# Five states of h·C on GpSimd in pairs, and the last stage in place

## The chip, the cores and the metric

The kernel runs on one core of one Trainium2 chip. The metric is the device time of one launch in microseconds (us), taken as the median of several runs. The engines are called as in the profile: PE (TensorE, the matrix engine; PEld is its weight load), ACT (ScalarE), DVE (VectorE), POOL (GpSimd) and SP (SyncE, which here issues all the DMAs).

## The reference

The input x is 8 images of 56x56 pixels with 192 channels, all in fp32. Two layers are applied, each as x + f(group_norm(x)).

Layer 0 is an attention with depthwise convolutions in front of its projections: 3 heads of 64, queries from all 3136 pixels, keys and values from a grid of 28x28.

Layer 1 is a two-dimensional selective scan. A projection gives 384 inner channels and a gate z. The inner channels go through a depthwise 3x3 convolution and a SiLU. Then four directions k (by rows, by columns, and both reversed) each run a recurrence with 16 states n for each channel d along the 3136 pixels l:

```python
def step(h, inp):
    u_l, d_l, B_l, C_l = inp
    dA = jnp.exp(d_l[..., None] * A)
    dBu = d_l[..., None] * B_l[:, :, None, :] * u_l[..., None]
    h = dA * h + dBu
    y = jnp.sum(h * C_l[:, :, None, :], axis=-1)
    return (h, y)
```

delta, B and C are projections of the input itself. The four y are put back into image order and summed, together with a skip term, normed over the channels, multiplied by silu(z), and projected back to 192 channels.

## The kernel before, in words

**Tiles.** The 384 inner channels lie in NJ = 3 blocks of 128 partitions. The 3136 pixels of an image are cut into NCH = 7 chunks of T = 448. A "step" is one chunk in one direction of one image: 8 x 4 x 7 = 224 steps, 28 to an image ("batch"). In a step the 16 states follow each other; the list `todo` holds all pairs (step i, state n). Chunks of the two reversed directions run from the last to the first, and each image ends with direction 2.

**A state of a step.**

- `row_loads`: SP loads row B_n of the chunk into all partitions (tile bb, 3 buffers) and, for states that POOL finishes, row C_n (tile cb, 2 buffers).
- `inputs_made`: POOL multiplies delta·u (du_s) by B into a tile h of 128 x 1344 (L1123). There are HBUFS = 7 of these tiles.
- `decays`: ACT makes da = exp(delta·A) in PSUM, once for each channel block (L1137, 2 buffers).
- `scans`: DVE scans the three blocks in place in h (L1154). `carries` copies the last column to the next chunk (newc, L1176).
- For 13 states, y gets h·C by way of PE and ACT. `turned`: PE transposes h in four parts of 112 pixels, three transposes each (ht, L1200). `scaled`: ACT copies each part with C as the scale of its partition (g, L1216, four for a state). `back`: PE transposes them back, adding into y in PSUM (L1234).
- For the three states in BY_POOL = (2, 7, 12), `by_pool` lets POOL do it: h·C for the three channel blocks (L1252; the first goes into tile yp, the others stay in h), and the addition of the second and third to yp (L1256). `summed` then has PE add yp to y by a matmul with the identity for each block (L1271). yp has one buffer.
- y is a single PSUM buffer of three banks. `evicted`: DVE adds it to yacc, which holds all 3136 pixels (L1288; with the skip term for direction 0, L1286), and y is free for the next step.

**Around a step.** `prepared` makes the delta of the coming step (L1063 to L1082 on PE, ACT and DVE), and POOL multiplies it by u (L1086). `skips` loads the skip input of the next image into yacc as soon as a chunk of yacc has been read. `finish` is the last stage of an image, one `part` for each chunk, from the last chunk to the first: the mean over channels by PE (L949), its subtraction into a tile yc (L951), square, variance, norm, gate (the product with silu(z) on POOL, L986), the output projection on PE (L996) and the store. `read[c]`, set in it, is what `skips` waits for. `front` and `x_proj` are layer 0 and the projections of layer 1 of the next image; they run beside the scans of the present one.

**The order.** Each of these functions is a generator. A planner (`Sched`) runs them all while the program is built: with a fixed cost for each operation it keeps a clock for each engine and gives the next place to the operation that could start earliest, less a rank. The order on each engine is thus fixed; on the chip the engines wait for each other by semaphores. Two limits steer it. `pace` ties the PE time spent on front to the number of states scanned. `ending` makes the last stage urgent while the count of `read` lags behind the chunks that are ready:

```python
def ending():
    done = sum(len(r) for r in yread.values())
    b, c = divmod(at["chunk"], NDIR * NCH)
    come = b * NCH + max(c - (NDIR - 1) * NCH, 0)
    return 1e9, 1e9 if done < come - 1 or done < b * NCH else 0.0
```

Where PE would have nothing to do, a filler puts in small matmuls with zeros (L1367).

Of the kernel before, what the change touches and what calls it, by code (L numbers as in the profile page):

```python
# [36 lines left out]
R = 12  # L37
NR = R + 2 * NST
NDIR = 4
BY_POOL = (2, 7, 12)  # L40
EPS = 1e-5
CAP = 60.0
HBUFS = 7
LEAD = 3


# [224 lines left out]
def kernel(  # L271
# [661 lines left out]
    def finish(b, gate, read):  # L933

        m = made[b]
        wz = yield c1("wz2", [CP, NB, DIN])
        yield from scaled_weights(wz.ap, wz.c[0], 1, m["rstd"], m["k_gn"])

        def part(c):
            cols = slice(c * T, (c + 1) * T)  # L940
            yv = yacc[:, :, cols]
            yield gate(c)
            yc = yield c1("yc", [128, NJ, T], parts=4)
            xt = yield c1("xt3", [CP, NB, T])
            yield from dma([m["k_x1"][c]], xt.c, 5.0, xt.ap, m["x1d"][:, :, cols])
            pmn = yield bank()
            for j in range(NJ):
                yield PE, t_mm(T), [k_y[c]], pmn.c if j == NJ - 1 else []
                nc.tensor.matmul(pmn.ap[:, :T], lnones, yv[:, j], start=(j == 0), stop=(j == NJ - 1))  # L949
            yield DVE, t_dve(NJ * T), pmn.c + [k_y[c]], [yc.c[0]]  # L950
            nc.vector.tensor_tensor(yc.ap, yv, pmn.ap[:, :T].unsqueeze(1).to_broadcast([128, NJ, T]), ALU.subtract)  # L951
            pmn.free()
            read[c] = True
            sz = yield c1("sz", [128, NJ, T], parts=NJ + 2)
            yield ACT, t_act(NJ * T), [yc.c[0]], [sz.c[0]]
            nc.scalar.activation(sz.ap, yc.ap, AF.Square)
            pvr = yield bank()
            for j in range(NJ):
                yield PE, t_mm(T), [sz.c[0]], pvr.c if j == NJ - 1 else []
                nc.tensor.matmul(pvr.ap[:, :T], lnones, sz.ap[:, j], start=(j == 0), stop=(j == NJ - 1))  # L960
            k1, k2 = Cell(), Cell()
            yield ACT, t_act(T), pvr.c, [k1]
            nc.scalar.activation(pvr.ap[:, :T], pvr.ap[:, :T], AF.Ln, bias=eps)
            yield ACT, t_act(T), [k1] + pvr.c, [k2]
            nc.scalar.activation(pvr.ap[:, :T], pvr.ap[:, :T], AF.Exp, scale=-0.5)
            for j in range(NJ):
                yield DVE, t_dve(T), [k2, yc.c[0]] + pvr.c, [yc.c[2]] if j == NJ - 1 else []
                nc.vector.scalar_tensor_tensor(yc.ap[:, j], yc.ap[:, j], lnw[:, j], pvr.ap[:, :T], ALU.mult, ALU.mult)
            pvr.free()
            for j in range(NJ):  # L970
                yield ACT, t_act(T), [yc.c[2]], [yc.c[1]] if j == NJ - 1 else []
                nc.scalar.activation(yc.ap[:, j], yc.ap[:, j], AF.Identity, bias=lnb[:, j])
            for j in range(NJ):
                pz = yield bank()
                yield PE, 2 * t_mm(T), xt.c + wz.c, pz.c
                for bl in range(NB):
                    nc.tensor.matmul(pz.ap[:, :T], wz.ap[:, bl, j * 128:(j + 1) * 128], xt.ap[:, bl],
                                     start=(bl == 0), stop=(bl == NB - 1))
                yield DVE, t_dve(T), pz.c + [m["k_nb"], k2], [sz.c[1 + j]]
                nc.vector.tensor_scalar(sz.ap[:, j], pz.ap[:, :T], m["nbias"][:, NJ + j:NJ + j + 1], None, ALU.add)  # L980
                pz.free()
            yield ACT, t_act(NJ * T) + 2.6, sz.c[1:1 + NJ], [sz.c[1 + NJ]]
            nc.scalar.activation(sz.ap, sz.ap, AF.Silu)
            nc.scalar.preload_act_table_set(EXP_LN)
            yield POOL, t_pool(NJ * T), [yc.c[1], sz.c[1 + NJ]], [yc.c[3]]
            nc.gpsimd.tensor_tensor(yc.ap, yc.ap, sz.ap, ALU.mult)  # L986
            sz.free()
            ot = yield c1("ot", [TP, SUB, C], parts=2)
            for s2_ in range(SUB // 2):
                po = yield bank()  # L990
                for i in range(2):
                    s = 2 * s2_ + i
                    tok = slice(s * TP, (s + 1) * TP)
                    yield PE, 3 * t_mm(C) + 0.25, [yc.c[3]] + xt.c, po.c if i else []
                    for j in range(NJ):
                        nc.tensor.matmul(po.ap[:TP, i * C:(i + 1) * C], yc.ap[:, j, tok], outpw[:, j],  # L996
                                         start=(j == 0), stop=False)
                    for bl in range(NB):
                        nc.tensor.matmul(po.ap[:TP, i * C + bl * CP:i * C + (bl + 1) * CP], xt.ap[:, bl, tok],
                                         ident[:CP, :CP], is_transpose=True, start=False, stop=(bl == NB - 1))  # L1000
                yield ACT, t_act(2 * C), po.c, [ot.c[s2_]]
                nc.scalar.copy(ot.ap[:, 2 * s2_:2 * s2_ + 2].rearrange("p s c -> p (s c)"), po.ap[:TP, :2 * C])
                po.free()
            yc.free()
            xt.free()
            yield from dma(ot.c, [], 4.5, out[b, cols, :].rearrange("(s p) c -> p s c", p=TP), ot.ap, [ot])

        for c in reversed(range(NCH)):
            yield from part(c)
        wz.free()  # L1010
# [4 lines left out]
    for b in range(nb):  # L1015

        for k in (0, 1, 3, 2):
            order = range(NCH) if k < 2 else range(NCH - 1, -1, -1)
            steps += [(b, k, c, i) for i, c in enumerate(order)]
    todo = [(i, n) for i in range(len(steps)) for n in range(NST)]  # L1020

    def view(t, j, k, c):

# [78 lines left out]
    def row_loads():  # L1102
        for i, n in todo:
            b, k, c, _ = steps[i]
            yield lambda: i in chunks
            m = made[b]
            cols = slice(c * T, (c + 1) * T)
            bb = yield s3("bb", [128, T])
            yield from dma([m["k_rows"][k, c]], bb.c, 3.2, bb.ap, m["rows"][k][R + n, cols].partition_broadcast(128))
            brow[i, n] = bb  # L1110
            if n in BY_POOL:
                cbr = yield s2("cb", [128, T])
                yield from dma([m["k_rows"][k, c]], cbr.c, 3.2, cbr.ap,
                               m["rows"][k][R + NST + n, cols].partition_broadcast(128))
                crow[i, n] = cbr
# [63 lines left out]
    def y_of(i):  # L1179

        if i not in ys:
            t = yield ry
            free = Cell()
            free.w = t.c[0].r
            at["y"] = i
            ys[i] = dict(t=t, free=free, on=False, left=[(NST - len(BY_POOL)) * SUB + 1] * NJ)
        return ys[i]

    def turned():

        for i, n in todo:
            if n in BY_POOL:
                continue
            yield lambda: (i, n) in states
            h = states[i, n][0]
            for s in range(SUB):
                ht = yield rht
                yield PE, t_turn(128), h.c[1:1 + NJ], ht.c
                for j in range(NJ):
                    nc.tensor.transpose(ht.ap[:TP, j * 128:(j + 1) * 128], h.ap[:, j, s * TP:(s + 1) * TP], ident)  # L1200
                turns[i, n, s] = ht
            over(i, n)

    turns, gs, yps = {}, {}, {}

    def scaled():
        for i, n in todo:
            if n in BY_POOL:
                continue
            for s in range(SUB):  # L1210
                yield lambda: (i, n, s) in turns
# [9 lines left out]

    def back():
        for i, n in todo:
            if n in BY_POOL:
                continue
            for s in range(SUB):
                yield lambda: (i, n, s) in gs
# [12 lines left out]
    def by_pool():  # L1240

        for i, n in todo:
            if n not in BY_POOL:
                continue
            yield lambda: (i, n) in states and (i, n) in crow and i in news
            h, cbr = states[i, n][0], crow.pop((i, n))
            if n == BY_POOL[0]:
                yp = yield s1("yp", [128, NJ, T], parts=NJ)
            to = yp if n == BY_POOL[0] else h
            for j in range(NJ):  # L1250
                yield POOL, t_pool(T), [h.c[1 + j], news[i].c[n]] + cbr.c, [to.c[j]] if to is yp else [h.c[1 + NJ + j]]
                nc.gpsimd.tensor_tensor(to.ap[:, j], h.ap[:, j], cbr.ap, ALU.mult)  # L1252
# [2 lines left out]
                yield POOL, t_pool(NJ * T), h.c[1 + NJ:] + yp.c, yp.c  # L1255
                nc.gpsimd.tensor_tensor(yp.ap, yp.ap, h.ap, ALU.add)  # L1256
            over(i, n)
            if n == BY_POOL[-1]:
                yps[i] = yp

    def summed():

        for i in range(len(steps)):
            yield lambda: i in yps
            yp = yps.pop(i)
            y = yield from y_of(i)
            yield lambda: y["left"][0] < (NST - len(BY_POOL)) * SUB
            for j in range(NJ):
                yield PE, t_mm(T), [yp.c[j]], []
                y["left"][j] -= 1  # L1270
                nc.tensor.matmul(y["t"].ap[:, j, :T], ident, yp.ap[:, j], start=False, stop=(y["left"][j] == 0))  # L1271
            yp.free()
# [166 lines left out]
```

## Time and profile before

| | |
|---|---|
| time, median of 3 runs | 19163.19 us (19162.22 to 19167.43) |
| profiled execution, its own time | 19161.15 us |
| its span, first to last instruction | 19159.4 us |
| granted PE clock, mean | 0.98 |
| busy: PE / DVE / ACT / POOL | 17257.6 / 14540.1 / 15414.1 / 15248.7 us |
| bytes moved by DMA | 1662 MB, 87 GB/s |

A profile page shows one execution. A group of instructions is a line of the kernel, an engine, an operation and its tiles (out<-in), with its count, its busy time, the mean duration of one, and the time that the engine stood idle before it, with what ended that wait. "issue" means that the profile shows nothing that was waited for. Matmuls are pipelined and an fp32 matmul leaves two records, a transpose one, so counts of PE and its busy share say less than those of the other engines. Views by window give the busy time of each engine in a stretch of the span.

### The profile page before, as it was taken

What the parts mean: (1) busy time and instruction counts of PE and PEld (TensorE: products, weight loads), DVE (VectorE), ACT (ScalarE), POOL (GpSimd) and SP (SyncE); (2) the same over time, 40 slices, a digit from 0 to 9 for tenths busy, and PEclk for the clock granted to TensorE, in tenths of its full rate; (3) what the DMA queues carried; (4) which work ended last, traced back from release to release, by engine and by line L of the source; (5) the groups of instructions that cost most, each with busy time, mean ns of one, the idle gap of its engine ahead of it and who ended that gap; (6) DMA issues with size and microseconds to landing.
All of it is one profiled execution on the core that took longest, in us unless ns stands there. A gap on an engine that the chain in (4) does not pass through costs nothing. (4 is left out here: it accounts for less than half of the span.)

```text
span 19159.4 us, 294576 instructions
## 1 busy us (share of the span) xinstructions
PE 17257.6 (90%) x105374; PEld 12258.8 (64%) x105374; DVE 14540.1 (76%) x19156; ACT 15414.1 (80%) x28166; POOL 15248.7 (80%) x6380
## 2 busy tenths in 40 slices
PE   8799988999889998899999999999998999988888
PEld 4466666666666666666666666666666666667776
DVE  2377777777777777777877777777787777778887
ACT  2478888788877888788887888878888788888887
POOL 0388888788877888788887888878888788889997
PEclk9899999999999999999999999999999999999999
DMA  1322223222332233322333223332233222332222
GB/s 51 116 79 72 89 90 111 76 74 87 98 110 72 76 94 95 104 76 73 99 97 98 75 79 94 101 94 75 78 94 115 82 75 78 93 110 75 75 76 63
DMA packets 1071987, 1662.15 MB, mean 87 GB/s; under 512 B 162244, under 2 KB 1054392, under 8 KB 1067448
## 3 DMA queue, kind: packets, MB, share of 16 engines
q1 hardware_dynamic: 1070520, 1643.29, 28.3%
q8 instruction: 835, 13.68, 0.3%
q14 instruction: 632, 5.18, 0.1%
HBM read 1455.13 MB, written 187.74 MB: 86 GB/s over the span
## 5 line engine op out<-in xcount | busy, mean ns | idle before, releaser
L1154 DVE TENSOR_TENSOR_SCAN h<-da,newc,h 128x448 f32<-128x448 f32 x9216 | 10121.3, 1137 | 2016.7 <-ACT da L1137 1150.6
L1123 POOL TENSOR_TENSOR h<-du_s,bb 128x1344 f32<-128x1344 f32 x3584 | 10834.3, 3051 | 883.6 <-PE ht L1200 644.8
L1216 ACT ACTIVATE g<-ht,ct_s 112x384 f32<-112x384 f32 x11648 | 6534.5, 577 | 1522.9 <-PE ht L1200 1430.9
L1137 ACT ACTIVATE da<-dl_s,acoef 128x448 f32<-128x448 f32 x10752 | 6758.4, 637 | 869.0 <-DVE h L1154 689.5
L1234 PE MATMUL y<-ident,g 112*128 112x112 f32 x34944 | 5481.1, 271 | 888.7 <-ACT g L1216 722.1
L1234 PEld LDWEIGHTS y<-ident,g 112*128 112x128 f32 x34944 | 3799.5, 143 | 3596.0 <-ACT g L1216 2874.9
L1200 PE MATMUL ht<-ident,h 128*112 128x128 f32 x34944 | 5652.8, 277 | 244.8 <-DVE h L1154 77.1
L1200 PEld LDWEIGHTS ht<-ident,h 128*112 128x112 f32 x34944 | 4017.1, 135 | 924.7 <-issue 413.5
L1252 POOL TENSOR_TENSOR h<-h,cb 128x448 f32<-128x448 f32 x1344 | 1492.5, 1141 | 1204.8 <-issue 1076.4
L1086 POOL TENSOR_TENSOR du_s<-dl_s,du_s 128x1344 f32<-128x1344 f32 x224 | 681.5, 3043 | 1662.5 <-DVE dl_s L1082 1529.8
L1154 DVE TENSOR_TENSOR_SCAN h<-da,h 128x448 f32<-128x448 f32 x1536 | 1608.3, 1079 | 432.3 <-ACT da L1137 280.1
L1367 PE MATMUL y<-zeros 128*128 128x64 f32 x13790 | 1886.8, 270 | 0.0
L1367 PEld LDWEIGHTS y<-zeros 128*128 128x128 f32 x13790 | 1804.9, 197 | 14.2 <-issue 14.2
L1256 POOL TENSOR_TENSOR yp<-yp,h 128x1344 f32<-128x1344 f32 x448 | 1367.1, 3052 | 7.6
L451 PE MATMUL bank<-xa,dg 128*128 128x440 f32 (+2 forms) x3024 | 1303.5, 538 | 72.6 <-ACT g L1216 46.1
L755 PE MATMUL bank<-qT,kT 128*112 128x448 f32 x2352 | 1099.1, 558 | 91.9 <-ACT pT L705 49.4
L764 PE MATMUL bank<-pT,vt 112*128 112x448 f32 x2352 | 1004.1, 545 | 79.6 <-ACT pT L705 55.5
L451 PE MATMUL bank<-band,dgq 96*96 96x440 f32 (+3 forms) x2016 | 830.3, 534 | 47.9 <-ACT g L1216 27.2
L705 ACT ACTIVATE pT<-bank,nsh 112x448 f32<-112x448 f32 x1176 | 743.8, 635 | 115.8 <-PE bank L755 100.9
L1252 POOL TENSOR_TENSOR yp<-h,cb 128x448 f32<-128x448 f32 x672 | 747.7, 1146 | 1.8 <-DVE h L1154 1.8
L1070 DVE SCALAR_TENSOR_TENSOR dl_s<-prep,e 128x448 f32<-128x448 f32 x672 | 410.1, 610 | 444.3 <-ACT e L1068 443.9
L1063 PE MATMUL prep<-dts,dtw 128*128 128x448 f32 x1344 | 653.5, 568 | 99.0 <-DVE dl_s L1082 65.4
(152 smaller groups left out, 12559.5 us busy)
## 6 DMA issues: line engine op xcount, KB each, us to landing
bb<-rows SPq DMA_DIRECT2D x3584, 224.0 KB
cb<-rows SPq DMA_DIRECT2D x672, 224.0 KB
xt<-x1d SPq DMA_DIRECT2D x224, 336.0 KB
du_s<-xch SPq DMA_DIRECT2D x112, 672.0 KB
du_s<-xcw SPq DMA_DIRECT2D x112, 672.0 KB
xch<-xv SPq DMA_DIRECT2D x24, 1568.0 KB
xcw<-xw SPq DMA_DIRECT2D x168, 224.0 KB
xs<-xch SPq DMA_DIRECT2D x56, 672.0 KB
```

The source lines that it names most:

```text
L451: nc.tensor.matmul(out[:, o0:o1, a:b], lhs, img(lo, hi)[:, :, a + dx - 1:b + dx - 1], start=(t == TAPS[0]), stop=(t == TAPS[-1]))
L755: nc.tensor.matmul(ps.ap[:TP, :T], kts[h][:, kb * TP:(kb + 1) * TP], qh.ap, start=True, stop=True)
L764: nc.tensor.matmul(po.ap[:, :T], vt[:, kb, g:g + 2, :].rearrange("p g d -> p (g d)"), pts[kb].ap, start=(kb == 0), stop=(kb == NKB - 1))
L1123: nc.gpsimd.tensor_tensor(h.ap, du.ap, bb.ap.unsqueeze(1).to_broadcast([128, NJ, T]), ALU.mult)
L1137: nc.scalar.activation(da.ap[:, :T], dl.ap[:, j], AF.Exp, scale=acoef[:, k * NJ + j, n:n + 1])
L1154: nc.vector.tensor_tensor_scan(h.ap[:, j, rev], da.ap[:, 0:T][:, rev], h.ap[:, j, rev], news[i - 1].ap[:, j, n:n + 1] if ci else 0.0, ALU. ...
L1200: nc.tensor.transpose(ht.ap[:TP, j * 128:(j + 1) * 128], h.ap[:, j, s * TP:(s + 1) * TP], ident)
L1216: nc.scalar.activation(g.ap, ht.ap[:TP, :DIN], AF.Copy, scale=ct.ap[:, s, n:n + 1])
L1234: nc.tensor.matmul(y["t"].ap[:, j, s * TP:(s + 1) * TP], g.ap[:, j * 128:(j + 1) * 128], ident[:TP, :TP], is_transpose=True, start=(n == 0 ...
L1252: nc.gpsimd.tensor_tensor(to.ap[:, j], h.ap[:, j], cbr.ap, ALU.mult)
L1256: nc.gpsimd.tensor_tensor(yp.ap, yp.ap, h.ap, ALU.add)
L1367: nc.tensor.matmul(ybanks[:, 0, T:T + FILL], zeros, zeros[:, :FILL], start=False, stop=False)
```

## The change

BY_POOL becomes two sets of groups. Steps of every image but the last use ((2, 5), (8, 10), (13,)); steps of the last image use ((2, 7), (12,)). Within a group, the first h·C goes into yp, the second is added to it, and with the last of the group yp is handed to PE, which adds it to y; `summed` now runs once for each group. The states that POOL finishes are left out of `turned`, `scaled` and `back`.

The last stage no longer has the tile yc: it works in place in its chunk of yacc (yv), and `read[c]` is set after the last output matmul instead of after the subtraction. The tile h, which has the size of yc, gets an eighth buffer.

```diff
-BY_POOL = (2, 7, 12)
+BY_POOL = (((2, 7), (12,)), ((2, 5), (8, 10), (13,)))
-HBUFS = 7
+HBUFS = 8
...
             yield gate(c)
-            yc = yield c1("yc", [128, NJ, T], parts=4)
+            kc = [Cell() for _ in range(4)]
...
-            nc.vector.tensor_tensor(yc.ap, yv, pmn.ap[:, :T].unsqueeze(1).to_broadcast([128, NJ, T]), ALU.subtract)
+            nc.vector.tensor_tensor(yv, yv, pmn.ap[:, :T].unsqueeze(1).to_broadcast([128, NJ, T]), ALU.subtract)
             pmn.free()
-            read[c] = True
...
-            nc.gpsimd.tensor_tensor(yc.ap, yc.ap, sz.ap, ALU.mult)
+            nc.gpsimd.tensor_tensor(yv, yv, sz.ap, ALU.mult)
...
-                    yield PE, 3 * t_mm(C) + 0.25, [yc.c[3]] + xt.c, po.c if i else []
+                    yield PE, 3 * t_mm(C) + 0.25, [kc[3]] + xt.c, po.c + [k_y[c]] if i else []
...
-            yc.free()
+            read[c] = True
             xt.free()
...
+    by = [BY_POOL[b < nb - 1] for b, *_ in steps]
+    by = [{n: (n == g[0], n == g[-1]) for g in groups for n in g} for groups in by]
...
-            if n in BY_POOL:
+            if n in by[i]:
                 cbr = yield s2("cb", [128, T])
...
-            ys[i] = dict(t=t, free=free, on=False, left=[(NST - len(BY_POOL)) * SUB + 1] * NJ)
+            ys[i] = dict(t=t, free=free, on=False, left=[(NST - len(by[i])) * SUB + sum(z for _, z in by[i].values())] * NJ)
...
-            if n == BY_POOL[0]:
+            first, last = by[i][n]
+            if first:
                 yp = yield s1("yp", [128, NJ, T], parts=NJ)
-            to = yp if n == BY_POOL[0] else h
+            to = yp if first else h
...
-            if n == BY_POOL[-1]:
-                yps[i] = yp
+            if last:
+                yps.append((i, yp))
...
-        for i in range(len(steps)):
-            yield lambda: i in yps
-            yp = yps.pop(i)
+        for _ in range(sum(z for d in by for _, z in d.values())):
+            yield lambda: yps
+            i, yp = yps.pop(0)
             y = yield from y_of(i)
-            yield lambda: y["left"][0] < (NST - len(BY_POOL)) * SUB
+            yield lambda: y["on"]
```

More of the change, by code (lines that the diff above doesn't have):

```diff
@@ L949, in part @@
                 nc.tensor.matmul(pmn.ap[:, :T], lnones, yv[:, j], start=(j == 0), stop=(j == NJ - 1))
-            yield DVE, t_dve(NJ * T), pmn.c + [k_y[c]], [yc.c[0]]
-            nc.vector.tensor_tensor(yc.ap, yv, pmn.ap[:, :T].unsqueeze(1).to_broadcast([128, NJ, T]), ALU.subtract)
+            yield DVE, t_dve(NJ * T), pmn.c + [k_y[c]], [kc[0]]
+            nc.vector.tensor_tensor(yv, yv, pmn.ap[:, :T].unsqueeze(1).to_broadcast([128, NJ, T]), ALU.subtract)
             pmn.free()
-            read[c] = True
             sz = yield c1("sz", [128, NJ, T], parts=NJ + 2)
-            yield ACT, t_act(NJ * T), [yc.c[0]], [sz.c[0]]
-            nc.scalar.activation(sz.ap, yc.ap, AF.Square)
+            yield ACT, t_act(NJ * T), [kc[0]], [sz.c[0]]
+            nc.scalar.activation(sz.ap, yv, AF.Square)
             pvr = yield bank()
@@ L966, in part @@
             for j in range(NJ):
-                yield DVE, t_dve(T), [k2, yc.c[0]] + pvr.c, [yc.c[2]] if j == NJ - 1 else []
-                nc.vector.scalar_tensor_tensor(yc.ap[:, j], yc.ap[:, j], lnw[:, j], pvr.ap[:, :T], ALU.mult, ALU.mult)
+                yield DVE, t_dve(T), [k2, kc[0]] + pvr.c, [kc[2]] if j == NJ - 1 else []
+                nc.vector.scalar_tensor_tensor(yv[:, j], yv[:, j], lnw[:, j], pvr.ap[:, :T], ALU.mult, ALU.mult)
             pvr.free()
             for j in range(NJ):
-                yield ACT, t_act(T), [yc.c[2]], [yc.c[1]] if j == NJ - 1 else []
-                nc.scalar.activation(yc.ap[:, j], yc.ap[:, j], AF.Identity, bias=lnb[:, j])
+                yield ACT, t_act(T), [kc[2]], [kc[1]] if j == NJ - 1 else []
+                nc.scalar.activation(yv[:, j], yv[:, j], AF.Identity, bias=lnb[:, j])
             for j in range(NJ):
@@ L984, in part @@
             nc.scalar.preload_act_table_set(EXP_LN)
-            yield POOL, t_pool(NJ * T), [yc.c[1], sz.c[1 + NJ]], [yc.c[3]]
-            nc.gpsimd.tensor_tensor(yc.ap, yc.ap, sz.ap, ALU.mult)
+            yield POOL, t_pool(NJ * T), [kc[1], sz.c[1 + NJ]], [kc[3]]
+            nc.gpsimd.tensor_tensor(yv, yv, sz.ap, ALU.mult)
             sz.free()
@@ L993, in part @@
                     tok = slice(s * TP, (s + 1) * TP)
-                    yield PE, 3 * t_mm(C) + 0.25, [yc.c[3]] + xt.c, po.c if i else []
+                    yield PE, 3 * t_mm(C) + 0.25, [kc[3]] + xt.c, po.c + [k_y[c]] if i else []
                     for j in range(NJ):
-                        nc.tensor.matmul(po.ap[:TP, i * C:(i + 1) * C], yc.ap[:, j, tok], outpw[:, j],
+                        nc.tensor.matmul(po.ap[:TP, i * C:(i + 1) * C], yv[:, j, tok], outpw[:, j],
                                          start=(j == 0), stop=False)
@@ L1191, in turned @@
         for i, n in todo:
-            if n in BY_POOL:
+            if n in by[i]:
                 continue
@@ L1202, in turned @@
             over(i, n)
-    turns, gs, yps = {}, {}, {}
+    turns, gs, yps = {}, {}, []
     def scaled():
         for i, n in todo:
-            if n in BY_POOL:
+            if n in by[i]:
                 continue
@@ L1223, in back @@
         for i, n in todo:
-            if n in BY_POOL:
+            if n in by[i]:
                 continue
@@ L1242, in by_pool @@
         for i, n in todo:
-            if n not in BY_POOL:
+            if n not in by[i]:
                 continue
```

## The prediction

> **What bounds the kernel now.** I read the page's part 1 first. PE 90%, ACT 80%, POOL 80%, DVE 76%: no engine is full over the span, and such averages mix stages. So I looked up in the timeline when the first scan (L1154) of each of the 224 steps starts. Batches 1 to 6, which share the engines with the next batch's first layer ("front"), take 2324 to 2329 us each, 83.1 us a step. The last batch has no front: 2015 us, and 68 to 71 us a step in its middle. Then I asked for the busy time of each engine in stretches of one middle batch (steps 7 to 15, which are attention; 18 to 23; 24 to 27, where the last stage runs; the whole batch) and in 18 steps of the last batch.
>
> ```profile
> core 0: us, PE busy (x) PEld busy (x) DVE busy (x) ACT busy (x) POOL busy (x), PEclk, DMA share, GB/s
> 8391.50:9116.10 724.60, 664.44 (x3859) 442.67 (x3857) 562.82 (x729) 632.50 (x1186) 605.18 (x253) 1.00 0.24 73
> 9282.30:9749.40 467.10, 422.89 (x2627) 299.30 (x2625) 374.33 (x479) 397.21 (x715) 403.12 (x169) 0.99 0.31 93
> 9749.40:10086.50 337.10, 306.24 (x1949) 225.85 (x1949) 260.44 (x341) 290.08 (x510) 281.33 (x117) 1.00 0.37 112
> 7759.70:10086.50 2326.80, 2114.86 (x12923) 1492.53 (x12922) 1819.98 (x2385) 1925.26 (x3520) 1906.52 (x797) 0.99 0.29 89
> 17321.00:18567.80 1246.80, 1085.95 (x8058) 893.98 (x8058) 1064.35 (x1369) 1077.32 (x2018) 1205.45 (x505) 0.96 0.25 75
> ```
>
> The last row: POOL is busy 1205 of 1247 us, 96.7%, and ACT 86%. POOL bounds the last batch. In attention ACT leads with 87%, POOL has 84%. Over the batch the two are level (1925 and 1907 us of 2327), and POOL stands idle for 420 us. The waits of that batch say why:
>
> ```profile
> PEld y L1234 <- ACT g L1216: 363.5, 837, 5.5
> DVE h L1154 <- ACT da L1137: 189.4, 233, 12.2
> ACT g L1216 <- PE ht L1200: 183.9, 269, 3.5
> POOL h L1252 <- issue: 149.2, 30, 15.4
> POOL du_s L1086 <- DVE dl_s L1082: 116.8, 18, 16.3
> POOL h L1123 <- PE ht L1200: 89.5, 35, 11.5
> ```
>
> PE waits for ACT, the scan waits for ACT, ACT waits for PE in turn: ACT stands in the middle. POOL's waits are of the other kind: for a scanned state (L1252), for the next step's delta (L1086), for a free h buffer (L1123). POOL is ahead and held up by the rest. PE's 90% is no bound: its rows are pipelined and hold 13,790 filler records (L1367). Counted at the rates shown below, its work in a middle batch is about 1690 us, 73%. The exception is step 3, with PE busy 114 of 120 us.
>
> **The change, by its parts.** The durations:
>
> ```profile
> L1216 ACT ACTIVATE g<-ht,ct_s 112x384 f32<-112x384 f32 x11648 | 6534.5, 577 | 1522.9 <-PE ht L1200 1430.9
> L1252 POOL TENSOR_TENSOR h<-h,cb 128x448 f32<-128x448 f32 x1344 | 1492.5, 1141 | 1204.8 <-issue 1076.4
> ...
> 17699.00 3.32 POOL L1252 TENSOR_TENSOR h<-h,cb 128x448 f32<-128x448 f32 x3
> 17705.28 3.04 POOL L1256 TENSOR_TENSOR yp<-yp,h 128x1344 f32<-128x1344 f32 x1
> ...
> 17703.88 0.82 PE L1200 MATMUL ht<-ident,h 128*112 128x128 f32 x6
> 17711.69 0.49 PE L1200 MATMUL ht<-ident,h 128*112 128x128 f32 x3
> ...
> 8011.28 2.42 PE L1271 MATMUL y<-yp,ident 128*128 128x448 f32 x6
> ```
>
> 1. Five states on POOL instead of three, in 196 of 224 steps (batches 0 to 6).
>  - ACT loses 2 x 4 copies g. 6534.5/11648 is 0.561 us each: 4.49 us a step, 126 us a batch.
>  - POOL gains 2 x 3 products. Three in a row take 3.32 us: +6.65. The adds stay two (2+5 and 8+10; before, 7 and 12 onto 2). +186 us a batch, on 1907.
>  - PE loses 2 x 24 transposes. Six take 0.82 and three 0.49 us, so 0.11 each: -5.3. It gains two more sums of three matmuls (six records, 2.42 us with the tail of the last, 2.25 without): +4.5. Net -0.8 us a step, 22 a batch: nothing to speak of where PE isn't full, 1 us in step 3.
> 2. The last batch (28 steps) keeps states 2, 7, 12 but drops the add behind 12: POOL -3.04 us a step, PE +2.25, which lies in time that fillers hold now.
> 3. h buffers 7 to 8. POOL waits 89.5 us a batch for one. I count this inside the stage estimates; alone it moves no work. If POOL becomes the bound, this wait goes by itself.
> 4. Two more loads of a C row a step on SP's queue, between the B rows, with still two "cb" buffers. cb(8) now waits for the product of state 2, and each later one for a product five or more states back (before: ten or more), and the next B rows queue behind it. POOL waits for B rows 173 us in the whole run now. Taken as 0: where POOL is ahead enough to be hit, it has idle time. Bounds 0 and twice today's wait, +173 us.
> 5. "yp" has one buffer and is filled three times a step. The product of 8 must wait for the matmuls of (2,5). Shown at 8011 us: the add ends at 8009.4, the matmuls at 8013.7, 4.3 us later; POOL has h inputs of 3.05 us each to make in between. Taken as 0; if such cover is missing, 4.3 us once or twice a step in the worst case.
> 6. The last stage in yacc. Its arithmetic and engines stay; "read" comes after the last output matmul instead of after the subtraction, and the next batch's yacc load on SP waits for that. In the boundary at 7780 us the subtraction of part 0 ended at 7844.7, the load was issued at once, and the eviction that needs it began at 7872.9. An urgent part takes some 41 us (part 1: 7797.7 to 7838.5), so with the same start the load would be issued at 7881 and the eviction come some 15 us late, behind which PE's y and the single y buffer queue. But the planner holds the stage urgent while "read" lags, and now that lasts to a part's end: parts that took 73 to 155 us from mean to output and started some 100 us after their chunk should each be done sooner, part 0 with them. Taken as 0, bounds -10 and +15 us at each of 7 boundaries. At the very end three parts are still open when the last chunk is evicted (19087.6, end 19159.4), about 27 us each: -15 us, bounds -27 and 0.
>
> **Two rules against it.** By the row POOL has idle time; by "Perfetto Trace Analysis" of the Trainium skill, section "Identifying the Most-Contended Engine", the engine of highest occupancy is the one to relieve. On the whole span ACT and POOL are level, and the change loads one of them: taken so, POOL's +6.65 x 196 less 3.04 x 28 would add 1218 us. I go by the stages (the same page grants regimes): POOL is full only where the change takes work off it. "SBUF — State Buffer", section "SBUF: two separate sides", says that VectorE with two SBUF inputs and a reading GpSimd exclude each other for whole instructions. If the scan fell under this, 6.65 us of new POOL work a step could hold it up, up to 1303 us in all. But it reads da from PSUM, and it lasts 1137 ns in the middle batch with POOL at 82% and 1139 in the last with POOL at 97%. No allowance.
>
> **The sum.** In a middle batch a stage gives at most ACT's 4.49 us a step, and not more than POOL allows at some 96% (the last row). Attention: 80.5 us a step now; POOL 67.2+6.65=73.9, over 0.96 is 77.0: -3.5 x 9 = -31. Steps 18 to 23: 77.9; POOL again 73.9, so 76.9: -1 x 6. Steps 24 to 27: 84.3; POOL 70.3+6.65, over 0.96 is 80.2: -4 x 4 = -16. Steps 0 to 2, 4 to 6, 16 and 17 are held by front chains: -2 each for the six, -1 each for the two, -14. Step 3: -1. Together -68, so -65 a batch with something left for points 4 and 5; 7 batches: -455. POOL would then be 93% busy there. Last batch: POOL is busy 67.0 of 69.3 us a step; 67.0-3.04 plus today's idle of 2.3 us gives 66.3; VectorE, at 59 us, is near, so -2.5 for 22 steps: -55. End: -15. In all -525 from the profiled 19161.15 (span 19159.4), which is 2 us below the median of 19163.19: about 18,640.
>
> **The rivals.**
> - POOL packs as in the last batch everywhere: 2093/0.967 = 2164 a batch, -163 x 7 - 70: about 17,950 at the end; half of it, 18,250, is likelier. For: its waits are for others. Against: front chains and step 3 leave holes that eight h buffers (half a step) can't bridge.
> - ACT's relief is eaten by the PE-ACT ping-pong (183.9 and 363.5 us of waits): only the last batch and the end gain, 19,090.
> - Slower: POOL waits in order. Each step now has five places, not three, where POOL stands at L1252 for a scan and can't make the next inputs. If that wait grows by 5/3 (149 to 248 us a batch) and the one at L1086 stays (117), a batch is 2093+365 = 2458: +131 x 7 - 70, about 20,000. It decides from 234 us of idle POOL a batch (2327-2093). Against: in the last batch, where POOL is behind, both waits are nearly nil.
> - No effect: gain and these waits cancel, 19,160.
>
> **How the numbers follow.** Main case 0.58, own range 18,400 to 18,880; packed 0.14; last batch only 0.16; no change 0.03; slower 0.09. Within 0.2% (38 us) counts as no change. The first three are faster: 0.88. The range 18,250 to 19,090 leaves out the slower case, most of no change and the far end of the packed one.
>
> **What would show it.** ACT's g falls from 11648 to 10080, h·C products rise from 2016 to 3192, sums on PE from 1344 to 3864 records. POOL's busy time should be near 16,470 us, 88%, L1252's "issue" wait below 1076, the scan's mean at 1137, a middle batch near 2262 and the last near 1960 us. A middle batch above 2327 with POOL below 90% would be the slower case; POOL above 95% in it, the packed one; fewer g and an unchanged batch would say that ACT was no bound.

## The result, and the profile after

The changed kernel takes 18863.91 us (median of 4 runs, 18845.24 to 18891.11) against 19162.81 us (4 runs): ratio 0.9845, 95% interval 0.9828 to 0.9862. It is 299 us faster; some 523 were forecast (18,640 us). Its profiled execution is the slowest of the four (18891.11 us, span 18889.4), 270 us below the one of before.

Cut by the first scan of each batch, those 270 us lie here:

| | before | after | forecast |
|---|---|---|---|
| start to first scan | 791.2 | 796.0 | - |
| batch 0 | 2312.9 | 2277.8 | -65 |
| batches 1 to 6, mean | 2326.7 | 2300.2 | -65 each |
| last batch | 2015.3 | 1957.2 | -55 |
| last scan to the end | 80.0 | 57.4 | -15 |

The last batch and the end came as forecast. The middle batches gave 26.5 us each, not 65. Part 1 of the page and the groups that the change touches (busy, mean ns, idle before):

```profile
PE 16973.1 (90%) x96640; PEld 11599.8 (61%) x96640; DVE 14534.5 (77%) x19156; ACT 14643.6 (78%) x26598; POOL 16416.5 (87%) x7528
L1219 ACT ACTIVATE g<-ht,ct_s 112x384 f32<-112x384 f32 x10080 | 5663.7, 576 | 1776.0 <-PE ht L1203 1701.2
L1256 POOL TENSOR_TENSOR yp<-h,cb 128x448 f32<-128x448 f32 x1932 | 2147.0, 1143 | 454.8 <-PE y L1275 216.6
L1256 POOL TENSOR_TENSOR h<-h,cb 128x448 f32<-128x448 f32 x1260 | 1399.1, 1141 | 291.3 <-issue 175.6
L1275 PE MATMUL y<-yp,ident 128*128 128x448 f32 x3864 | 1594.0, 547 | 5.1 <-POOL yp L1260 4.5
```

Counts and busy times are those of the working: 10080 copies g, 3192 products, 3864 records of sums, POOL at 16,417 us (16,470 forecast). The work moved as costed. What the moved work was worth in time is where the forecast missed. The same stretches of a middle batch as before (attention; steps 18 to 23; 24 to 27; the whole batch) and steps 3 to 20 of the last:

```profile
core 0: us, PE busy (x) PEld busy (x) DVE busy (x) ACT busy (x) POOL busy (x), PEclk, DMA share, GB/s
8295.10:8997.80 702.70, 655.04 (x3548) 418.31 (x3546) 559.37 (x728) 597.25 (x1114) 662.07 (x308) 1.00 0.30 81
9172.50:9646.10 473.60, 433.04 (x2414) 289.99 (x2412) 371.80 (x481) 381.44 (x671) 446.47 (x206) 0.98 0.34 99
9646.10:9979.70 333.60, 297.65 (x1756) 217.64 (x1757) 262.33 (x347) 274.05 (x484) 305.48 (x141) 0.95 0.40 116
7679.20:9979.70 2300.50, 2087.63 (x11788) 1414.10 (x11786) 1809.88 (x2385) 1815.64 (x3296) 2085.17 (x965) 0.97 0.33 96
17107.20:18304.40 1197.20, 1057.64 (x7609) 851.50 (x7610) 1063.45 (x1369) 1066.29 (x2015) 1152.16 (x487) 0.96 0.27 78
```

ACT fell from 1925 to 1816 us a batch, POOL rose from 1907 to 2085 (91%); the batch shortened by a quarter of ACT's relief. A step of attention takes 78.1 us (77.0 forecast), of steps 18 to 23 78.9 (76.9; it was 77.9), of 24 to 27 83.4 (80.2). The waits of that batch:

```profile
ACT g L1219 <- PE ht L1203: 238.5, 286, 10.8
DVE h L1157 <- ACT da L1140: 183.9, 207, 11.0
DVE h L1157 <- POOL h L1126: 156.1, 68, 6.3
ACT da L1140 <- DVE h L1157: 123.8, 217, 4.0
POOL du_s L1089 <- DVE dl_s L1085: 71.7, 9, 19.7
POOL h L1126 <- DMA bb<-rows: 40.3, 10, 9.7
POOL yp L1256 <- PE y L1275: 32.9, 7, 9.0
```

Of the waits before, the forecast shows all but these two:

```profile
DVE h L1154 <- POOL h L1123: 124.6, 48, 6.3
ACT da L1137 <- DVE h L1154: 82.6, 153, 5.1
```

POOL's waits for scans and h buffers are nearly gone. In their place the scan waits longer for POOL (156 us; 125 before), and ACT longer for PE and for the scan (239 and 124; 184 and 83). Most of ACT's freed time became ACT's waiting time.

### The profile page after: what moved, and what is told of

It is laid out like the page before. It is cut to its first block, busy times and chain, and to the rows that moved or that the text cites. A ratio compares the mean times of both kernels' runs of the same rounds, so it can differ in the third digit from the quotient of the medians.

```text
span 18889.4 us, 274433 instructions
## 1 busy us (share of the span) xinstructions
PE 16973.1 (90%) x96640; PEld 11599.8 (61%) x96640; DVE 14534.5 (77%) x19156; ACT 14643.6 (78%) x26598; POOL 16416.5 (87%) x7528
## 5 line engine op out<-in xcount | busy, mean ns | idle before, releaser
L1157 DVE TENSOR_TENSOR_SCAN h<-da,newc,h 128x448 f32<-128x448 f32 x9216 | 10111.4, 1136 | 2166.1 <-ACT da L1140 1155.7
L1219 ACT ACTIVATE g<-ht,ct_s 112x384 f32<-112x384 f32 x10080 | 5663.7, 576 | 1776.0 <-PE ht L1203 1701.2
L1237 PE MATMUL y<-ident,g 112*128 112x112 f32 x30240 | 4742.3, 271 | 660.2 <-ACT g L1219 506.3
L1237 PEld LDWEIGHTS y<-ident,g 112*128 112x128 f32 x30240 | 3305.9, 143 | 3236.8 <-ACT g L1219 2466.3
L1203 PE MATMUL ht<-ident,h 128*112 128x128 f32 x30240 | 4935.7, 277 | 287.4 <-DVE h L1157 87.4
L1203 PEld LDWEIGHTS ht<-ident,h 128*112 128x112 f32 x30240 | 3481.3, 135 | 1064.4 <-issue 450.9
L1256 POOL TENSOR_TENSOR yp<-h,cb 128x448 f32<-128x448 f32 x1932 | 2147.0, 1143 | 454.8 <-PE y L1275 216.6
L1371 PE MATMUL y<-zeros 128*128 128x64 f32 x11944 | 1651.3, 272 | 0.0
L1371 PEld LDWEIGHTS y<-zeros 128*128 128x128 f32 x11944 | 1586.1, 198 | 48.6 <-issue 48.6
L1275 PE MATMUL y<-yp,ident 128*128 128x448 f32 x3864 | 1594.0, 547 | 5.1 <-POOL yp L1260 4.5
L1275 PEld LDWEIGHTS y<-yp,ident 128*128 128x128 f32 x3864 | 701.3, 193 | 551.6 <-issue 505.2
```

The lines of the kernel that those rows point to most:

```text
L1157: nc.vector.tensor_tensor_scan(h.ap[:, j, rev], da.ap[:, 0:T][:, rev], h.ap[:, j, rev], news[i - 1].ap[:, j, n:n + 1] if ci else 0.0, ALU. ...
L1219: nc.scalar.activation(g.ap, ht.ap[:TP, :DIN], AF.Copy, scale=ct.ap[:, s, n:n + 1])
L1237: nc.tensor.matmul(y["t"].ap[:, j, s * TP:(s + 1) * TP], g.ap[:, j * 128:(j + 1) * 128], ident[:TP, :TP], is_transpose=True, start=(n == 0 ...
L1371: nc.tensor.matmul(ybanks[:, 0, T:T + FILL], zeros, zeros[:, :FILL], start=False, stop=False)
```

## The experiments

Lengths of batches below are from the profiled execution of each kernel: the mean of batches 1 to 6, and the last. For the two kernels above they are 2327 and 2015, 2300 and 1957.

**Which part of the change.** e1 keeps the last stage in place and the eighth buffer, with three states in one group:

```diff
-BY_POOL = (((2, 7), (12,)), ((2, 5), (8, 10), (13,)))
+BY_POOL = (((2, 7, 12),), ((2, 7, 12),))
```

> The changed kernel with the three old states in one group again (2, 7, 12) in every image; the in-place last stage and the eighth h buffer stay. Theory A (GpSimd has become the bound of the middle batches, and ACT's relief is what paid there): middle batches back near 2315 to 2327 us, the last batch back near 2015, only the end shorter by some 20 us: 19,080 to 19,150. Rival B (the eighth buffer or the longer urgency of the last stage brought the gain of the middle batches, not the moved states): middle batches stay near 2300, 18,930 to 18,980.

Measured: 19296 us, ratio 1.0068 (1.0052 to 1.0085), slower than before; middle batches 2354, the last 2035. Both expectations were wrong, but B far more: buffer and last stage did not bring the gain. Kinds and numbers of instructions are those of before, yet a middle batch is 27 us longer. The planner made the order anew around the two edits and around the new condition for `summed`; which of them costs the 27 us was not taken apart.

e2 moves the states alone; the whole of `part` is that of before:

```diff
-HBUFS = 8
+HBUFS = 7
...
-            kc = [Cell() for _ in range(4)]
+            yc = yield c1("yc", [128, NJ, T], parts=4)
...
-            yield lambda: y["on"]
+            yield lambda: "all" in y
```

> The moved states alone: five states in the groups of the change, but the last stage with its own tile and seven h buffers as before. (Two lines of the order's bookkeeping are added so that the sums of a group wait for the whole first state in y.) Theory A: most of the gain is here, middle batches near 2300, last near 1950, the end as before: 18,880 to 18,930. Rival B: middle batches near 2327, only the last batch gains: about 19,100.

Measured: 18894 us, ratio 0.9863 (0.9848 to 0.9878); 2298 and 1971, and 81 us from the last scan to the end, as before. The states are the gain of the middle batches and give 44 of the last batch's 58 us; the other 14, and the 23 us of the end, come with the rest of the change. Attention and steps 18 to 23 of one of its middle batches, in the columns of the rows above:

```profile
8306.40:9000.10 693.70, 649.99 (x3521) 417.22 (x3519) 559.72 (x728) 596.58 (x1114) 662.51 (x307) 1.00 0.28 82
9176.80:9626.30 449.50, 417.42 (x2430) 284.74 (x2429) 369.35 (x480) 378.46 (x668) 441.70 (x205) 1.00 0.34 103
```

The work is that of the changed kernel, whose batch is as long. The stages are not: here POOL is busy 95.5% and 98% in them, and they are 9 and 24 us shorter than there; the other steps are longer.

e3 splits the three states into two groups in every image:

```diff
-BY_POOL = (((2, 7), (12,)), ((2, 5), (8, 10), (13,)))
+BY_POOL = (((2, 7), (12,)), ((2, 7), (12,)))
```

> The changed kernel with the three states (2, 7), (12,) in every image: against e1 it takes one add of 3.04 us a step off GpSimd and puts 2.25 us of matmuls on PE; ACT's work is that of before. Theory A: in the middle batches of three states GpSimd is no bound, so they give at most 1 us a step (0 to -30 a batch); the last batch gives 55: about 18,950 to 19,080. Rival C (GpSimd was the bound in the middle batches before as well): -3 us a step everywhere, 18,450 to 18,550.

Measured: 19226 us, ratio 1.0037 (1.0022 to 1.0052); 2347 and 1968. Against e1 the middle batches give 8 us, the last 67. With three states POOL is no bound of the middle batches: rival C falls. The absolute time missed because e1's did.

e6 takes the eighth buffer out of the changed kernel (`HBUFS = 7`):

> The changed kernel with seven h buffers instead of eight. e1 (three states, in place, eight buffers) came out 0.7% above the kernel before, so one of the two has a price. Theory F (the eighth buffer lets the plan run GpSimd further ahead and costs): faster than the changed kernel, 18,720 to 18,800. Rival G (the longer urgency of the in-place last stage costs): within 40 us of the changed kernel or slower, 18,830 to 18,950. Forecast's own view (a buffer more can only help): 18,900 to 19,000.

Measured: 18855 us, ratio 0.9846 (0.9826 to 0.9867); 2297 and 1956. The eighth buffer is worth nothing here. With five states the in-place stage costs nothing in all either (e2 against e6: 18894 and 18855). That leaves the order as the likely cause in e1; it is argued, not shown.

**What a microsecond of an engine's work is worth.** The next four change one engine's load and leave the planned order, the semaphores and all other work as they were. The "share" of an engine is the time gained or lost for each microsecond of its work that is taken or added. e5 halves the adds to yp in the changed kernel, e10 in the kernel before:

```diff
-                nc.gpsimd.tensor_tensor(yp.ap, yp.ap, h.ap, ALU.add)
+                nc.gpsimd.tensor_tensor(yp.ap[:, :, :T // 2], yp.ap[:, :, :T // 2], h.ap[:, :, :T // 2], ALU.add)
```

> The changed kernel with every add of a pair (h to yp) over the first 224 of 448 columns only, so that half of the second product of a pair is left out of y. Instructions, waits and their order stay; GpSimd is relieved of about 3.0 us a step in batches 0 to 6 and 1.5 in the last. Theory A: a middle batch falls by 1.5 to 2.5 us a step, 2230 to 2258 us, 18,400 to 18,600 in all. Rival D (waits of the fixed order hold GpSimd, its load does not matter): middle batches stay within 10 us of 2300, 18,780 to 18,850.

> The kernel before, with both adds to yp over the first 224 of 448 columns only (half of the products of states 7 and 12 is left out of y): GpSimd is relieved of about 3.0 us a step, nothing else is moved. Theory A (GpSimd bounds the last batch alone): last batch -45 to -60, middle batches -5 each at most: 19,070 to 19,120. Theory E (a share of 0.1 to 0.28 in the middle batches too): middle batches -8 to -24 each, 18,930 to 19,060. Rival C (bound everywhere): 18,560 to 18,650.

e9 (kernel before) and e11 (changed kernel) make two of the four copies g of a state in two halves:

```diff
-                nc.scalar.activation(g.ap, ht.ap[:TP, :DIN], AF.Copy, scale=ct.ap[:, s, n:n + 1])
+                for part in ((0, DIN // 2), (DIN // 2, DIN)) if s % 2 == 0 else ((0, DIN),):
+                    nc.scalar.activation(g.ap[:, part[0]:part[1]], ht.ap[:TP, part[0]:part[1]], AF.Copy,
+                                         scale=ct.ap[:, s, n:n + 1])
```

> The kernel before, with the copy g of sub-blocks 0 and 2 of a state made in two halves: 26 more ACT instructions a step, some 4.2 to 5.2 us of ACT, about what the change takes off it; order, waits and all other engines stay. Theory A (ACT sets the pace of most middle steps): +3 us or more a step there, +20 in the last batch, 19,650 to 20,000. Theory E (no engine is the bound alone; at a fixed order each one's load counts by a share, ACT's being 0.3 to 0.5): 19,400 to 19,650. Rival H (ACT's load does not matter): below 19,260.

> The changed kernel with the same split of g: 22 more ACT instructions a step, some 3.5 to 4.4 us. Theory A (after the change GpSimd bounds the middle batches and ACT has slack): at most +1 us a step, 18,880 to 19,060. Theory E (ACT's share stays at 0.3 to 0.5): 19,080 to 19,280. Rival H: below 18,920.

Measured:

| | time, us | ratio to before | middle batch | last batch |
|---|---|---|---|---|
| e5, after, POOL less | 18772 | 0.9798 (0.9783 to 0.9813) | 2279 | 1955 |
| e10, before, POOL less | 19129 | 0.9979 (0.9972 to 0.9987) | 2323 | 2005 |
| e9, before, ACT more | 19613 | 1.0235 (1.0220 to 1.0250) | 2384 | 2078 |
| e11, after, ACT more | 19180 | 1.0007 (1.0000 to 1.0014) | 2333 | 2016 |

The size of each push is read from the profile: the row of g in e9 and then e11 (busy), and part 1 of e5 and then e10 (POOL).

```profile
L1217 ACT ACTIVATE g<-ht,ct_s 112x192 f32<-112x192 f32 (+1 forms) x17472 | 7418.2, 479 | 1400.4 <-PE ht L1200 1334.0
```

```profile
L1220 ACT ACTIVATE g<-ht,ct_s 112x192 f32<-112x192 f32 x15120 | 6427.7, 478 | 1667.8 <-PE ht L1203 1611.1
```

```profile
PE 16918.4 (90%) x96640; PEld 11570.5 (62%) x96640; DVE 14473.3 (77%) x19156; ACT 14636.1 (78%) x26598; POOL 15821.3 (84%) x7528
```

```profile
PE 17240.2 (90%) x105374; PEld 12244.8 (64%) x105374; DVE 14511.0 (76%) x19156; ACT 15402.3 (81%) x28166; POOL 14614.2 (76%) x6380
```

g is busy 883.7 us longer in e9 (7418.2 less 6534.5), 110 a batch, and the middle batch grew by 58: a share of 0.52. In e11 it is 764.0 us, 93 a middle batch (22 of the split copies in each of its steps, 26 in those of the last), for 32: 0.35. POOL lost 595 us in e5, 79 a middle batch (two adds a step there, one in the last), for 21: 0.27. In e10 it lost 634, 79 a batch, for 3: 0.04. So ACT's work counted by half before and counts by a third now; POOL's went from next to nothing to a quarter.

These are rough figures. ACT's work is counted here by the rows of g, as in the forecast; by the busy time of all of ACT, in which neighbouring records overlap, the pushes are 88 and 77 us a middle batch and the shares 0.65 and 0.42. Each length is that of one profiled execution, and that of the changed kernel is 27 us above its median, that of e5 13 below: by the medians of the whole run, e5 gains 92 us for 595, a share of 0.15, so POOL's share after the change lies somewhere from 0.15 to 0.27. And ACT's work was only added, never taken away.

Theory A (POOL now bounds, ACT is free) fails in e5 and e11 as a statement on the whole batch. Rival D (load does not matter) comes close in time, but its middle batches should have stayed within 10 us and fell by 21. Theory E, formed after e5, holds in e9 and e11; in e10 the middle batches do what A expected and the last batch what nobody did.

A share of a batch is a mean over stages. Divided at the first scans of the steps and averaged over batches 1 to 6, the length of a stage, and behind the stroke the busy time of the engine pushed, changed by (us):

| steps | the change | forecast | e9, ACT more, before | e11, ACT more, after | e5, POOL less, after |
|---|---|---|---|---|---|
| 0 to 6 | -16.1 | -13 | 12.1 / 23.0 | 6.4 / 19.7 | -6.8 / -21.1 |
| 7 to 15, attention | -20.4 | -31 | 19.3 / 27.6 | 15.0 / 24.5 | -0.9 / -25.4 |
| 16 and 17 | 6.4 | -2 | 5.5 / 6.4 | 0.1 / 6.0 | -1.0 / -5.7 |
| 18 to 23 | 9.9 | -6 | 12.1 / 19.2 | 1.2 / 16.4 | -10.8 / -15.5 |
| 24 to 27, last stage | -6.3 | -16 | 8.6 / 12.0 | 9.8 / 10.5 | -1.7 / -11.3 |

In e10 no row moves by more than 1.2 us. Attention in one middle batch of e5 and of e11, to be set against the changed kernel's 702.70 us above:

```profile
8242.70:8944.70 702.00, 654.68 (x3548) 418.37 (x3546) 559.08 (x729) 597.30 (x1114) 636.69 (x307) 1.00 0.28 81
8410.20:9127.50 717.30, 667.14 (x3548) 421.98 (x3547) 562.53 (x728) 621.82 (x1309) 662.11 (x307) 1.00 0.29 80
```

There POOL is busy 94% and ACT 85%, yet 25 us less of POOL's work gave 1 us, and 24 us more of ACT's cost 15: the busier engine does not set the pace. In steps 18 to 23 it seems to be the other way round, with shares of 0.70 for POOL and 0.07 for ACT. That pair is loose, since these steps vary from 466 to 488 us between the batches of the changed kernel.

**The last batch.** e10 gave it 10 us for 79 us less POOL work, the change 58 for 85. e12 is e10 with the halved cost told to the planner:

```diff
-                yield POOL, t_pool(NJ * T), h.c[1 + NJ:] + yp.c, yp.c
+                yield POOL, t_pool(NJ * T // 2), h.c[1 + NJ:] + yp.c, yp.c
```

> e10 again (the kernel before with half of each add to yp, half of two products left out of y), but the planner is told: the add's cost in it is halved too, so the order on all engines is made anew for a lighter GpSimd. In e10, with the old order, the last batch fell by only 10 us for 83 us of relief, while the changed kernel's last batch fell by 58 for the same relief. Theory O (the written-out order, not only GpSimd's load, sets the last batch's pace; it has to be made for the lighter engine): last batch 1950 to 1980. Rival P (the last batch is bound by ACT and PE and the change gained there by its third sum or otherwise): last batch 2000 to 2012. Middle batches by either: 2310 to 2345.

Measured: 19103 us, ratio 0.9972 (0.9961 to 0.9982); 2329 and 1966. Theory O holds: with an order made for the lighter POOL the last batch falls by 49 us, with the old order by 10. In e9 the same batch grew by 62 us for 110 of ACT. So even a POOL at 96.7% did not set the pace alone there; which of the reordered instructions matter was not tried.

**Single waits.** e13 gives the C rows five buffers, e7 gives yp two; both take the room from the eighth h buffer:

```diff
-                cbr = yield s2("cb", [128, T])
+                cbr = yield s2("cb", [128, T], 5)
```

```diff
-                yp = yield s1("yp", [128, NJ, T], parts=NJ)
+                yp = yield s2("yp", [128, NJ, T], parts=NJ)
```

> The changed kernel with five buffers for the C rows instead of two, their room taken from the eighth h buffer (seven h buffers alone, e6, cost nothing). In the changed kernel SP's queue stands some 250 us of a middle batch in front of a C row whose buffer GpSimd still holds, with B rows and the other image's loads queued behind. Theory Q (this queue is what eats GpSimd's time: waits for B rows 40 us and for the first layer's loads): middle batches 2255 to 2280, 18,560 to 18,740. Theory E (shares, no single wait): within 50 us of the changed kernel, 18,810 to 18,910.

> The changed kernel with two buffers for yp, their room taken from the eighth h buffer. GpSimd waits 217 us in the changed kernel for PE to read yp. Theory Y (the single yp buffer costs what it shows): -150 to -220 us, 18,640 to 18,720. Theory E (the wait lies where GpSimd has a share of 0.28 in the time): -20 to -70, 18,790 to 18,850.

SP's own waits in a middle batch of the changed kernel:

```profile
SPq L467 <- POOL h L1126: 1154.7, 344, 20.3
SPq L467 <- POOL yp L1256: 131.9, 39, 9.7
SPq L467 <- POOL h L1256: 120.5, 24, 14.7
```

The first is SP in front of a B row's buffer, the lower two in front of a C row's. In e13 neither is among the long waits any more and POOL waits for B rows 127 us in the whole run, not 246. The time: 18849 us, ratio 0.9836 (0.9822 to 0.9851), batches of 2293 and 1958, 15 us less than the changed kernel and within the intervals of both. Theory Q falls. e7: 18929 us, ratio 0.9877 (0.9862 to 0.9892), 2305 and 1962, 65 us slower than the changed kernel. The wait for yp went, and POOL's waits for a scanned state came back:

```profile
POOL h L1256 <- issue: 253.8, 80, 11.0
POOL h L1256 <- DVE newc L1179: 230.6, 76, 8.4
```

In both runs the theory of the single wait failed; e13 came out as theory E expected, e7 outside both. A wait that was taken away was no gain here. Both runs also have a new order, so what a wait costs by itself is not shown.

**A faster version.** e14 is e13 with every state of POOL in a group of its own, so that POOL adds nothing:

```diff
-BY_POOL = (((2, 7), (12,)), ((2, 5), (8, 10), (13,)))
+BY_POOL = (((2,), (7,), (12,)), ((2,), (5,), (8,), (10,), (13,)))
```

> e13 (five C-row buffers, seven h buffers) with every state of GpSimd a group of its own: no adds at all; PE adds each product to y. (The two bookkeeping lines of e2 are in.) GpSimd is relieved of 6.1 us a step in batches 0 to 6 and 3.0 in the last, PE gets 4.5 and 2.25 us more. Theory E with GpSimd's share of 0.28 and none for PE: 18,500 to 18,600. With a share of PE of about 0.3 as well: 18,730 to 18,820. Rival R (five hand-overs through one yp buffer eat it): 18,850 to 18,950 or more. It is also the candidate for a kernel faster than both.

Measured: 18762 us, ratio 0.9798 (0.9785 to 0.9811): faster than both kernels, 0.5% below the changed one. Middle batches 2280, the last 1933. Against e13 that is 12 us for 170 us less POOL work in a middle batch. PE's 126 us more, the hand-overs and the new order are what can have taken the rest. The wait for yp in e13 and in e14:

```profile
POOL yp L1256 <- PE y L1275: 177.1, 49, 9.1
POOL yp L1259 <- PE y L1278: 692.8, 176, 12.0
```

How much is PE's load was not measured by itself.

## Why the forecast was right, and where it was not

- **Direction and range: right.** Taking g from ACT pays, POOL has room for most of the work, and the number lies in the range, 16 us inside the slow end of the main case. The case of "only the last batch and the end" did not come: the seven other batches give 194 of 270 us.
- **The cost of each part: right.** The counts came out as stated. The rows of g fell by 124 us a batch (126 forecast) and those of the products rose by 187 (186); in the busy time of the whole engines, where records overlap, it is 107 and 179. PE's small net can't be read from its pipelined rows.
- **The worth of ACT's relief in a middle batch: mis-sized.** The sum let it count in full (4.49 us a step) until POOL reached 96%, and POOL at nothing until then; that gave 65 us a batch, and 26.5 were measured. The runs show part prices from the start: for the batch 0.52 falling to 0.35 for ACT, 0.04 rising to 0.15 to 0.27 for POOL. With the means of each pair and 0.27, 0.44 x 126 less 0.16 x 186 gives 26 us. That close agreement is partly luck: PE's load is not in it, and it does not hold in every stage. Worked by stage with the table's figures it gives -22 in attention, where ACT lost 35 us and POOL gained 57, and +11 in steps 18 to 23, with 16 and 43 (-20 and +10 measured), but -8 in steps 0 to 6 and -11 in 24 to 27 (-16 and -6 measured).
- **POOL's ceiling of 96%: not what held attention.** POOL stopped at 94% there, and making it lighter gained nothing (e5). Yet in the order of e2 it reached 95.5% and 98% in attention and in steps 18 to 23, and over six batches they took 77.1 and 75.5 us a step (77.0 and 76.9 forecast). There the shortfall lies in the other steps: the sum gave them -31 us, in e2 they are 16 us longer than before. Which instructions hold them is open.
- **Steps 0 to 3: right by luck.** -7 was forecast and -12 measured, but as +22 in steps 0 to 2 and -34 in step 3. e1, with three states, shifts the same way (+33 and -40), and e2, without the in-place stage, about half as far (+14 and -17). No single part of the change is the reason.
- **The slower case was near.** It was to decide from 234 us of idle POOL a batch; 2300.5 less 2085.2 is 215. POOL's idle time in front of the products shrank (1207 us in the whole run before, 746 now; on "issue" 1076 and 314), as argued from the last batch. Waits for B rows (246 us, 173 before) and for yp (217) took part of its place.
- **The last batch: right number, half the reason.** 58 us (55 forecast), 66.5 us a step (66.3). POOL's lighter load at the old order was worth 10 us (e10), with the order made anew for it 49 (e12), and 14 of the 58 come only with the rest of the change (e2). The sum had neither the order nor that in it; that it hit is partly luck.
- **yacc in place: right on the load and the end.** At the boundary after batch 2 part 0's last matmul ended at 7756.3, the skip load was issued then, and the eviction began at 7787.5, 31 us later (28 before). Parts of the middle batches take 41 to 110 us (41 to 155 before, one 178), those of that batch start 6 to 76 us after their chunk instead of about 100, and the end lost 23 us (15 forecast).
- **Points 4 and 5 at zero: not contradicted.** SP does stand in front of the C rows, 252 us a middle batch, as point 4 said. The cover of point 5 was often missing: POOL waits for yp 217 us in all. Removing either gained nothing in a new order (e13, e7).
- **The eighth buffer** was left inside the estimates; it is worth nothing (e6).
- **The two rules of the Trainium skill.** "Perfetto Trace Analysis", section "Identifying the Most-Contended Engine", takes occupancy as the measure of which engine to optimize first. Here occupancy was not the share by which an engine counts: over the whole span ACT and POOL stood level at 80% with shares of 0.52 and 0.04, and in attention after the change the busier one counted less (e5, e11). For the port shared by VectorE and GpSimd ("SBUF — State Buffer", section "SBUF: two separate sides") the scan's mean is 1136 ns with POOL at 87% (1137 before): no sign of it.

```profile
L1157 DVE TENSOR_TENSOR_SCAN h<-da,newc,h 128x448 f32<-128x448 f32 x9216 | 10111.4, 1136 | 2166.1 <-ACT da L1140 1155.7
```

## What to carry to other kernels

Where four engines are some 75 to 90% busy and wait for each other in turn, give no engine the full price of its work: stretch or shorten one engine's instructions at the same order, and read the price as time gained over work taken, stage by stage. Here moving work paid roughly by the difference of two such shares, and both moved towards each other as work was moved. In a kernel whose order is written out by a planner, an edit also makes a new order; here equal work came out up to 27 us a batch apart, which a forecast has to keep in its range.

## What was not expected of the hardware

The mean granted clock fell from 0.980 to 0.971. The trace has only two levels, full and half; at half clock PE spent 764 us before and 1094 after, in the middle batch shown 58 and 123 us. 65 us more at half clock take 33 us of PE's capacity, near the shortfall of 38.5 a batch, though by the forecast's estimate PE's work fills only 73% of a batch. e14 spends 658 us at half clock and e13 862, at nearly the same time for a batch; the kernel before is slower than both. Whether the clock cost anything here was not isolated and stays open.
